# A one-core kernel of a sparse attention layer and a ranked non-local layer: GpSimd takes some relus, scaled sums and squares, mask products follow the relus, ranking tiles become fixed pieces, and the planner's preferences are set anew

## The chip, the cores and the metric

One core of a Trainium2 chip runs the whole program. The metric is the device time in microseconds (us) of one execution. TensorE is called PE here, VectorE DVE, ScalarE ACT, GpSimd POOL and SyncE SP, as in the profile. All data are float32 except some masks and throw-away outputs.

## What is computed

The input x is 2 images of 256 channels and 64x64 = 4096 pixels. Layer 0: a 3x3 convolution to 64 channels, a batch norm and a PReLU give e; the similarity of all pixels, e^T e, is put through a sparsemax along each row (subtract a threshold tau, relu), and x times that matrix is added to x. Layer 1: every pixel gets a vector g of 128 channels and two numbers a and b; y at pixel n is the sum over m of relu(a_n + b_m) g_m / 4096; y is projected back to 256 channels, scaled by a batch norm, and added to the input of the layer.

```
y = where(bn(conv(x)) >= 0, ., prelu * .);  e = y.reshape(B, 64, 4096)
p = relu(sim - tau)          # sim = e^T e, tau: sparsemax threshold of the row
x = x @ p + x
f = relu(a[:, None] + b[None, :]);  y = (f / 4096) @ g
out = bn(wz @ y) + x
```

## The kernel before, in words

**Survey, list, rows.** The kernel counts on almost every row of the sparsemax having one non-zero entry, its own pixel. For each image a *survey* (`survey`, L475) forms the similarity in units of 128 rows by 1024 columns: PE multiplies (L472), DVE keeps a running maximum over the columns (`columns`, L499: a copy L501 for the first row tile, a maximum L503 for the others), ACT sums what lies over the row's limit (L507). The limits come from `thresholds` (L419): PE turns e, ACT copies it, DVE squares (L448) and sums it. `listed` (L580) lists the at most 512 rows that need more, fetches them by indirect DMAs of POOL, and a mask marks all other pixels. `rows` (L728) computes the listed rows in 4 tiles k of 128 rows by 4 column pieces q: PE product, ACT copy to z (L745), DVE top 8 (L748). When the four pieces are there, DVE's `threshold` (L750 to L762; L754 in it is a subtraction on 128x8) gives the bias, and a `relu` (L765) of each 128x1024 piece of z runs on ACT (L768) or on DVE (L770). `doubled` (L713) multiplies x by the mask on POOL, 8 pieces of 128x1024 for each image (L720). `attend` (L787) multiplies z by the fetched columns of x on PE (L794), and DVE adds that into x (L801), for which the piece's mask product must be done.

**Layer 1.** `project` and `project_in` give g, a and b (`ga`). Instead of the full sum, keys b are *ranked* (class `Ranked`): for image 0 all 32 tiles of 128 keys, for image 1 the first 16 tiles. The rank of each key in a tile t is counted by `above` against all keys (L992 on ACT with Sign and a running sum, or L997 on DVE), in two instructions, the keys before and behind the tile, and `ties` (L1004, DVE) counts equal keys inside the tile. `place` adds the counts up, `scatter` writes the tile's rows of `ga` to DRAM in the order of the ranks (an indirect DMA of POOL, L1026). `chain` then loads the sorted table, makes prefix sums (L1052, L1059, L1066), stores them, finds for every pixel the place of its a (`segments` L1086/L1087 on DVE, L1095 on PE, `counts`), and fetches one row of the table per pixel (64 indirect DMAs of POOL, L1112). `scaled_sums` (L1125, DVE) combines its halves, PE turns the result (L1132), and `finish` (L900) projects it with PE (L912), adds x on DVE (L916) and sends it out. The last 16 tiles of keys of image 1 go the direct way: ACT makes f = relu(a + b_m) of 128x1024 (`pair_f`, L1397, 64 of them), PE sums f against g (`pair_py`, L1407), ACT scales the result (L1418).

**The order of the work.** Nothing of it is an order by hand. `Plan` (L94) is a list scheduler that runs while the program is built: every `plan.task` has a cost in us on each engine that may take it (P = PE, D = DVE, A = ACT, G = POOL, S = SP), a rank (its preference; the lower goes first), tasks it comes after, and rings of buffers it takes and frees. At each step the engine that can begin first takes the task that would be least late, and of these the one with the lowest rank; a task with two costs goes to whichever engine picks it first. Instructions are issued in that order, and each engine's queue runs in order on the chip. The costs decide nothing but the order.

**Rings and rooms.** PSUM has 3 buffers of 1024 columns (`ring_sim`) and 2 of 512 (`ring_av`). f has 4 buffers in SBUF, which `ring_f` tells the planner of. Large SBUF rooms S0 to S6 are used several times; `kb` and `tab` of image 0 lie where its z was, and `rest` (L1418) where the throw-away output `junk` of ranking 0 was.

Of the kernel before, what the change touches and what calls it, by code (L numbers as in the profile page):

```python
# [19 lines left out]
P = 128  # L20
# [5 lines left out]
CT = 2  # L26
# [164 lines left out]
def sparse_path(ctx: ExitStack, tc, a, out, rows_i):  # L191
# [88 lines left out]

    plan = Plan()
    ring_sim, ring_av, ring_y, ring_b, ring_f = Ring(3), Ring(2), Ring(2), Ring(2), Ring(4)
# [136 lines left out]
    def thresholds(b, e_of, there, rank):  # L419
# [21 lines left out]

        def limits(jp):
            if jp == 0:
                for n in ("d", "thr", "nthr", "lim"):
                    both[n] = small.tile([P, NT], F32, name=f"{n}_{b}", tag=n, bufs=2)
            es = d[jp, "es"]
            sq = work.tile([P, 2, 4, CR], F32, name=f"sq_{b}_{jp}", tag="wb")
            nc.vector.tensor_mul(sq, es, es)  # L448
            c = both["d"][:, ts(jp, 8)]
            nc.vector.tensor_reduce(c, sq, AX.X, ALU.add)  # L450
            thr = both["thr"][:, ts(jp, 8)]
            nc.vector.tensor_scalar(thr, c, 1.0 - SLACK_REL, -1.0 - SLACK, ALU.mult, ALU.add)
            nc.vector.tensor_scalar_mul(both["nthr"][:, ts(jp, 8)], thr, -1.0)
            lim = both["lim"][:, ts(jp, 8)]
            nc.vector.tensor_scalar(lim, c, 1.5 * SLACK_REL, 1.0 + 1.5 * SLACK, ALU.mult, ALU.add)

        limited, saved = [], []
        for jp in range(NCB // 2):
# [3 lines left out]
            u = plan.task({"D": 2.1}, lambda jp=jp: limits(jp), rank, [t], take=hb, free=[hb])  # L462
            limited.append(u)
            saved.append(plan.task({"S": 0.2}, lambda jp=jp: stored(jp), rank, [t, u], lat=2.6, free=[hy]))
# [10 lines left out]
    def survey(b, e_of, both, there, copied, limited, accs, rank, ready):  # L475
# [23 lines left out]
        def columns(i, q, acc):  # L499
            if i == 0:  # L500
# [28 lines left out]
        def one_unit(i, q):  # L529
# [8 lines left out]
            if q == i // 8:  # L538
                rest.append(plan.task({"D": 1.32, "A": 1.3}, lambda e: own_row(e, i, q), r, [t, limited[i // 8]], free=[h]))
                return  # L540
            acc = accs[q % len(accs)]
            before = [first] + (turns.get(q - len(accs), []) if i == 0 else [chain[q]])
            u = plan.task({"D": 1.3}, lambda: columns(i, q, acc), r, [t, *before])
            chain[q] = u
            rest.append(plan.task({"A": 1.3}, lambda: rows_over(i, q), r, [u, limited[i // 8]], free=[h]))
# [32 lines left out]
        return plan.task({"D": 1.5}, listing, rank - 1, rest + limited), lambda: got_s["flag"], pes  # L578

    def listed(b, et, flag_of, saved, flagged, got, rank, free_mask, free_ec):  # L580
# [116 lines left out]
        pl = T({"D": 4.0}, places, rank, [t], free=[h])  # L697
# [30 lines left out]
    def rows(b, e_of, got, ecs, rank, free_z):  # L728
# [36 lines left out]
        def relu(e, k, q):  # L765
# [3 lines left out]
            else:  # L769
                nc.vector.tensor_scalar(z, z, nbs[k], 0.0, ALU.add, ALU.max)  # L770

        done, pes = {}, []
        for k in range(KB):
# [8 lines left out]
            t = plan.task({"D": 2.0}, lambda k=k: threshold(k), rank - 0.2, tops)  # L782
            for q in range(NU):
                done[k, q] = plan.task({"A": 1.16, "D": 0.8}, lambda e, k=k, q=q: relu(e, k, q), rank - 0.1, [t])
# [115 lines left out]
    def finish(b, cols, scaled, engine, rank, after, free):  # L900
# [27 lines left out]
        for ct in range(CT):  # L928
            t = plan.task({"D": 0.68}, lambda ct=ct: last(ct), rank, [ps[ct]], free=[hz] if ct == CT - 1 else [])
            plan.task({"S": 0.05}, lambda ct=ct: out_of(ct), 50, [t])  # L930

    class Ranked:
# [8 lines left out]
        def __init__(self, b, ga, R, at):  # L941
            self.b, self.ga, self.R, self.at = b, ga, R, at
            self.key = None if ga is None else ga[:, 0:R, CI + 1]
            self.lo, self.hi = 0, R
            self.placed = self.found = 0

        def keys(self):
# [16 lines left out]
            self.junk = None  # L964
            self.cnt = small.tile([P, R, 4], F32, name=f"cnt_{b}", tag=f"cnt{b}")
            nc.vector.memset(self.cnt[:, 0, 0:1], 0.0)
            nc.vector.memset(self.cnt[:, :, 2], 0.0)
# [14 lines left out]
        def above(self, t, on_act):  # L982

            if self.junk is None:
                self.junk = self.at("junk", [P, 2, self.R * P], BF16)
            kb, cnt = self.kb, self.cnt
            n = self.R * P
            for d, (c0, c1) in enumerate(((0, t * P), (t * P, n))):
                if c0 == c1:
                    continue  # L990
                if on_act:
                    nc.scalar.activation(  # L992
                        self.junk[:, 0, c0:c1], kb[:, c0:c1], AF.Sign, scale=STEEP,
                        bias=self.bound[:, d, t : t + 1], accum_out=cnt[:, t, d : d + 1],
                    )
                else:
# [3 lines left out]
                    )  # L1000

        def ties(self, t):

            nc.vector.scalar_tensor_tensor(  # L1004
                self.junk[:, 1, ts(t, P)], self.kb[:, ts(t, P)], self.key[:, t : t + 1], low,
                ALU.is_equal, ALU.mult, accum_out=self.cnt[:, t, 3:4],
            )

        def place(self, t0, n, on_act):

            b, R = self.b, self.R
            cnt = self.cnt[:, ds(t0, n)]
            if on_act:

                nc.vector.memset(cnt[:, :, 2], float(R * P))
            rk = small.tile([P, 4], F32, name=f"rk_{b}_{t0}", tag="rk", bufs=2)
            nc.vector.tensor_reduce(rk[:, 0:n], cnt[:, :, 0:3], AX.X, ALU.add)
            nc.vector.scalar_tensor_tensor(
                self.rank[:, ds(t0, n)], rk[:, 0:n], 0.5 if on_act else 1.0, cnt[:, :, 3], ALU.mult, ALU.add
            )  # L1020
# [98 lines left out]
        def taken(self, i, rank, rest=None):  # L1119
# [3 lines left out]
            def scaled_sums(t):  # L1123
                rt = self.r[:, t % TH]
                nc.vector.scalar_tensor_tensor(  # L1125
# [16 lines left out]
            for t in mine:  # L1142
                u = plan.task({"D": 0.3}, lambda t=t: scaled_sums(t), rank, [self.fetched[t]])
                u = plan.task({"P": 0.14}, lambda t=t: turned(t), rank, [u] + ([v] if t % 4 else []), take=None if t % 4 else h)
                v = u
                if t + TH < NT:
                    self.fetch_task(t + TH, rank, [u])
# [3 lines left out]
        def fetch_task(self, t, rank, after):  # L1151
            self.fetched[t] = plan.task({"G": 1.02}, lambda: self.fetch(t), rank, after, lat=4.14)

        def begin(self, rank, after, ranked, chained, then, room):

            self.chained, self.then, self.ranked = chained, then, ranked
            self.parts = {"D": [], "A": []}
            self.places_done, self.aboves, self.over = [], [], plan.gate()
# [4 lines left out]
            n = self.R / NT  # L1163
            for t in range(self.R):
                self.aboves.append(
                    plan.task(
                        {"D": 4.55 * n, "A": 4.15 * n}, lambda e, t=t: self.ranked_by(e, t),
                        lambda e, t=t: ranked + (t if e == "D" else self.R - t) / 100.0, [sp, *room],
                    )
                )  # L1170

        def ranked_by(self, e, _):
            t = self.hi - 1 if e == "A" else self.lo
            self.lo, self.hi = (self.lo, t) if e == "A" else (t + 1, self.hi)
            self.above(t, e == "A")
            me = self.aboves[_]
            tie = plan.task({"D": 0.3}, lambda: self.ties(t), self.ranked - 0.6, [])
            mine = self.parts[e]
            mine.append((t, me, tie))
            for x, m in self.parts.items():  # L1180
                if m and (len(m) == 4 or self.lo == self.hi):
                    t0, k = min(y[0] for y in m), len(m)
                    deps = [y[1] for y in m] + [y[2] for y in m]
                    pl = plan.task({"D": 0.5 if x == "A" else 0.3}, lambda t0=t0, k=k, x=x: self.place(t0, k, x == "A"), self.ranked - 0.7, deps)
                    for i in range(t0, t0 + k):
                        self.places_done.append(plan.task({"G": 1.02}, lambda i=i: self.scatter(i), self.ranked, [pl], lat=2.3))
                    m.clear()
            if self.lo == self.hi:
                self.chain()

        def chain(self):

            R, b, rk, H = self.R, self.b, self.chained, self.R // TH
            plan.let_go(self.over, self.places_done)
# [5 lines left out]
            for i in range(R // 2):  # L1200
                t = plan.task({"D": 0.82}, lambda i=i: self.sums(2 * i, 2 * i + 2), rk + 0.5, [t])
# [637 lines left out]
```

## Time and profile before

| | us |
|---|---|
| median of 3 runs | 735.35 (734.71 to 736.77) |
| the profiled execution | 737.18 |
| its span, first to last instruction | 735.4 |
| busy: PE / DVE / ACT / POOL | 636.2 / 559.1 / 398.2 / 203.5 |
| granted clock of PE, mean | 0.938 |

The profile's page names lines of the kernel (L754 is line 754) and groups of instructions with their mean length. A view of windows cuts the span into stretches with the busy time of each engine; a timeline lists one engine's instructions with start, length, and in brackets the idle time before them and what ended it; a view of waits adds such idle times up. In the span the stages lie about so: conv of image 0 to 60, survey 0 and conv of image 1 to 200, rows 0 to 262, survey 1 with attend 0 in between to 350, rows 1 with the rest of attend 0 to 440, attend 1 and ranking 0 to 520, ranking 0 and 1 with the pairs to 600, chains, fetches and pairs to 690, the last of `finish` to the end.

### The profile page before, as it was taken

What the parts mean: (1) busy time and instruction counts of PE and PEld (TensorE: products, weight loads), DVE (VectorE), ACT (ScalarE), POOL (GpSimd) and SP (SyncE); (2) the same over time, 40 slices, a digit from 0 to 9 for tenths busy, and PEclk for the clock granted to TensorE, in tenths of its full rate; (3) what the DMA queues carried; (4) which work ended last, traced back from release to release, by engine and by line L of the source; (5) the groups of instructions that cost most, each with busy time, mean ns of one, the idle gap of its engine ahead of it and who ended that gap; (6) DMA issues with size and microseconds to landing.
All of it is one profiled execution on the core that took longest, in us unless ns stands there. A gap on an engine that the chain in (4) does not pass through costs nothing.

```text
span 735.4 us, 8191 instructions
## 1 busy us (share of the span) xinstructions
PE 636.2 (87%) x2783; PEld 312.3 (42%) x2783; DVE 559.1 (76%) x1025; ACT 398.2 (54%) x552; POOL 203.5 (28%) x252
## 2 busy tenths in 40 slices
PE   5989979999876979999897959996798998979683
PEld 4656444444322323333544524445443644534341
DVE  6875787677788998786746485999999987772463
ACT  0122647766555877666031352999999865414010
POOL 0006930000048000000083000152445323777240
PEclk9999999999979899999998969998899899979898
DMA  9512010001021000000110002011425345654364
GB/s 353 185 43 59 2 29 15 15 15 30 15 65 29 1 1 1 0 1 0 59 37 0 0 1 115 8 37 37 138 99 136 98 159 201 218 162 107 129 226 152
DMA packets 32984, 54.75 MB, mean 74 GB/s; under 512 B 12850, under 2 KB 19876, under 8 KB 32036
## 3 DMA queue, kind: packets, MB, share of 16 engines
q1 hardware_dynamic: 27252, 40.60, 16.5%
q0 software_dynamic: 5248, 12.94, 6.5%
q10 hardware_dynamic: 432, 0.59, 0.3%
q8 instruction: 24, 0.39, 0.2%
q14 instruction: 28, 0.23, 0.1%
HBM read 31.94 MB, written 20.07 MB: 71 GB/s over the span
## 4 chain that ended last, share of the span: by engine, by line
PE 50%; DVE 23%; ACT 12%; issue 6%; POOL 4%; DMA 4%; DVEq 0%; ACTq 0%; POOLq 0%; SPq 0%
PE sv L472 16%; ACT junk L992 9%; PE av L794 7%; PE cv_in L362 6%; PE cv_out L362 6%; PE py L1407 4%; DVE junk L997 4%; POOL r L1112 4%; DVE mq L748 4%; DVE xbs L503 4%; PE pz L912 3%; PE g L825 2%; DVE z L754 2%; DMA r<-tb,k 2%; DVE z L770 2%
## 5 line engine op out<-in xcount | busy, mean ns | idle before, releaser
L507 ACT ACTIVATE sv<-sv,nthr 128x1024 f32<-128x1024 f32 x134 | 145.9, 1090 | 93.7 <-DVE xbs L503 47.8
L472 PE MATMUL sv<-e 64*128 64x512 f32 x640 | 162.7, 627 | 7.3 <-ACT sv L507 7.3
L794 PE MATMUL av<-z,xbs 128*128 128x512 f32 x256 | 124.2, 627 | 15.5 <-DVE z L770 15.0
L503 DVE TENSOR_TENSOR xbs<-sv,xbs 128x1024 f32<-128x1024 f32 x90 | 110.1, 1224 | 29.6 <-PE sv L472 24.2
L1407 PE MATMUL py<-f,ga 128*128 128x512 f32 x256 | 120.7, 624 | 3.4 <-ACT f L1397 3.4
L992 ACT ACTIVATE junk<-kb,bound 128x640 bf16<-128x640 f32 (+30 forms) x58 | 96.5, 1665 | 8.7 <-DMA kb<-rd_k 8.7
L1397 ACT ACTIVATE f<-ab,ga 128x1024 f32<-128x1024 f32 x64 | 71.3, 1142 | 47.3 <-PE py L1407 47.2
L472 PEld LDWEIGHTS sv<-e 64*128 64x128 f32 x640 | 55.7, 189 | 92.6 <-ACT sv L507 49.9
L1026 POOL DMA_INDIRECT sg<-ga,rank x48 | 49.9, 1041 | 148.3 <-DVE junk L1004 104.0
L794 PEld LDWEIGHTS av<-z,xbs 128*128 128x128 f32 x256 | 47.5, 197 | 82.4 <-issue 55.6
L1112 POOL DMA_INDIRECT r<-tb,k x64 | 61.2, 957 | 59.1 <-PE yr L1132 20.7
L997 DVE TENSOR_SCALAR_CACHE_REDUCE junk<-kb,ga 128x128 bf16<-128x128 f32 (+29 forms) x36 | 76.6, 2162 | 0.2
L666 POOL DMA_INDIRECT eb<-et,idx x8 | 7.9, 983 | 243.8 <-DVE idx L660 129.2
L1407 PEld LDWEIGHTS py<-f,ga 128*128 128x128 f32 x256 | 49.5, 200 | 59.8 <-issue 52.7
L362 PE MATMUL cv_out<-v,wu 128*64 128x256 f32 (+1 forms) x384 | 48.8, 397 | 7.4 <-DVE v L324 7.4
L362 PE MATMUL cv_in<-v,wu 128*64 128x256 f32 (+1 forms) x384 | 49.0, 398 | 4.9 <-DVE col L524 3.9
L1125 DVE SCALAR_TENSOR_TENSOR r<-r,a 128x128 f32<-128x128 f32 x64 | 21.6, 350 | 31.3 <-DMA r<-tb,k 31.0
L801 DVE SCALAR_TENSOR_TENSOR x<-av,b,x 128x512 f32<-128x512 f32 x32 | 23.7, 747 | 27.7 <-PE av L794 26.1
L745 ACT COPY z<-rw 128x1024 f32<-128x1024 f32 x32 | 30.5, 1026 | 26.1 <-PE av L794 17.3
L362 PEld LDWEIGHTS cv_out<-v,wu 128*64 128x64 f32 x384 | 30.4, 142 | 29.0 <-issue 12.5
L912 PE MATMUL pz<-yT,wz_sb 128*128 128x512 f32 x64 | 33.3, 662 | 9.4 <-DVE yT L1139 8.1
L512 DVE MAX8 top<-sv 128x8 f32<-128x1024 f32 x26 | 32.0, 1231 | 12.2 <-PE sv L472 11.8
(202 smaller groups left out, 752.4 us busy)
## 6 DMA issues: line engine op xcount, KB each, us to landing
out<-x SPq DMA_DIRECT2D x32, 256.0 KB, 2.1
tb<-tab SPq DMA_DIRECT2D x3, 2056.0 KB
x<-in_x SPq DMA_DIRECT2D x8, 512.0 KB, 8.7
tab<-sg SPq DMA_DIRECT2D x3, 1040.0 KB, 7.6
x<-in_x SPq DMA_DIRECT2D x4, 544.0 KB
e<-e SPq DMA_DIRECT2D x16, 128.0 KB, 3.2
et<-es SPq DMA_DIRECT2D x16, 128.0 KB, 1.9
mask<-kd SPq DMA_DIRECT2D x2, 1024.0 KB, 4.6
```

Of the source, the lines that this page charges most:

```text
L362: nc.tensor.matmul(d[jp, g][ts(h, CR), n, (r0 - r) * HH : (r1 - r) * HH], lhsT=taps(j, kc, dy), rhs=v[:, kc, r0 + dy - 1 : r1 + dy - 1], s ...
L472: nc.tensor.matmul(ps[:, ts(h, CB)], lhsT=lhs(h), rhs=e[ts(h, CR), q], start=True, stop=True)
L503: nc.vector.tensor_tensor(out=acc, in0=d[i, q], in1=acc, op=ALU.max)
L507: nc.scalar.activation(ps, ps, AF.Relu, bias=both["nthr"][:, i : i + 1], accum_out=got_s["over"][:, i, q : q + 1])
L794: nc.tensor.matmul(pss[j, ct], lhsT=got["xb"][:, k, ts(ct, P)], rhs=got["zs"][k][:, ts(j, CB)], start=(k == 0), stop=(k == KB - 1),)
L912: nc.tensor.matmul(d["z"][:, ct], lhsT=wz_sb[:, ts(ct, P)], rhs=d["y"], start=True, stop=True)
L992: nc.scalar.activation(self.junk[:, 0, c0:c1], kb[:, c0:c1], AF.Sign, scale=STEEP, bias=self.bound[:, d, t : t + 1], accum_out=cnt[:, t, d ...
L997: nc.vector.tensor_scalar(self.junk[:, 1, c0:c1], kb[:, c0:c1], self.key[:, t : t + 1], None, (ALU.is_ge, ALU.is_gt)[d], ALU.add, accum_ou ...
L1026: rows = nc.gpsimd.indirect_dma_start(out=self.sg, out_offset=bass.IndirectOffsetOnAxis(ap=self.rank[:, t : t + 1], axis=0), in_=self.ga[: ...
L1112: nc.gpsimd.indirect_dma_start(out=self.r[:, t % TH], out_offset=None, in_=self.tb, in_offset=bass.IndirectOffsetOnAxis(ap=self.k[:, t : t ...
L1397: nc.scalar.activation(f[0][:, m % 4, :], ab1[0][:, ts(q, UN)], AF.Relu, bias=ga1[0][:, m, CI : CI + 1])
L1407: nc.tensor.matmul(pys[q][:, ts(h, CB)], lhsT=ga1[0][:, m, 0:CI], rhs=f[0][:, m % 4, ts(h, CB)], start=(m == NR), stop=(m == NT - 1),)
```

## The change

- **Squares**: L448 moves from DVE to POOL, as a task of its own between the ACT copy and the limits.
- **First columns**: the copy of the first row tile (L501) may go to ACT.
- **Relus of z** may also go to POOL, at a planner's cost of 1.3 (`GF`).
- **Mask products** come after all 16 relus of the image (`done.values()`), no longer only after the mask.
- **f** of the pairs may go to POOL as well; the ring of f and the strict order of the f tasks are replaced by a dependence on the fourth `pair_py` back.
- **Scaled sums** may go to POOL, as two instructions (a product and an addition).
- **Ranking tiles as fixed pieces**: before, the engine that took a ranking task chose the tile (ACT from the top end down, DVE from the bottom up), and four tiles of the same engine were placed together. Now each task has its tile, goes to ACT or DVE, and tiles 4i to 4i+3 are placed together; ACT's counts get columns of their own (3 and 4), so `place` has two reductions and a memset for each tile that ACT took.
- **Preferences**: twenty ranks are set anew, and some costs in the planner are nearer to lengths (fetch 1.02 to 1.27, scatter 1.02 to 1.28, turns 0.14 to 0.27). A fetch also waits for the counts of its tile.

```diff
+    GF = 1.3
+    DB, CV1, LS, RW0, SV1, RW1, A0, G0, A1, R0, K0, CH0, R1, K1, CH1, P1, P2, SP1, PY, PF = 6.7, 13.3, -11.03, -18.93, -8.67, 0.74, -7.78, -1.83, -12.57, 4.87, 15.62, -10.51, -8.38, -10.32, 14.63, -1.37, -22.58, -8.67, 14.89, -20.4
+    other = {"D": nc.vector, "G": nc.gpsimd}
...
+        def squared(jp):
+            es = d[jp, "es"]
+            d[jp, "sq"] = work.tile([P, 2, 4, CR], F32, name=f"sq_{b}_{jp}", tag="wb")
+            nc.gpsimd.tensor_mul(d[jp, "sq"], es, es)
...
-            u = plan.task({"D": 2.1}, lambda jp=jp: limits(jp), rank, [t], take=hb, free=[hb])
+            v = plan.task({"G": 1.1}, lambda jp=jp: squared(jp), rank, [t], take=hb)
+            u = plan.task({"D": 1.2}, lambda jp=jp: limits(jp), rank, [v], free=[hb])
...
+            if e == "A":
+                nc.scalar.copy(acc, d[i, q])
...
-                nc.vector.tensor_scalar(z, z, nbs[k], 0.0, ALU.add, ALU.max)
+                other[e].tensor_scalar(z, z, nbs[k], 0.0, ALU.add, ALU.max)
...
-                done[k, q] = plan.task({"A": 1.16, "D": 0.8}, lambda e, k=k, q=q: relu(e, k, q), rank - 0.1, [t])
+                done[k, q] = plan.task({"A": 1.16, "D": 0.8, "G": GF}, lambda e, k=k, q=q: relu(e, k, q), rank - 0.1, [t])
...
+        def place(self, t0):
+
+            b = self.b
+            for t in range(t0, t0 + 4):
+                if t in self.on_act:
+                    nc.vector.memset(self.cnt[:, t, 0:1], float(self.R * P // 2))
+            cnt = self.cnt[:, ds(t0, 4)]
+            rk = small.tile([P, 2, 4], F32, name=f"rk_{b}_{t0}", tag="rk", bufs=2)
+            nc.vector.tensor_reduce(rk[:, 0], cnt[:, :, 0:3], AX.X, ALU.add)
+            nc.vector.tensor_reduce(rk[:, 1], cnt[:, :, 3:5], AX.X, ALU.add)
+            nc.vector.scalar_tensor_tensor(self.rank[:, ds(t0, 4)], rk[:, 1], 0.5, rk[:, 0], ALU.mult, ALU.add)
...
+                if e == "G":
+                    nc.gpsimd.tensor_scalar_mul(rt[:, 0:CI], rt[:, 0:CI], self.a[:, 0, t : t + 1])
+                    nc.gpsimd.tensor_add(rt[:, 0:CI], rt[:, 0:CI], rt[:, CI + 1 : CS])
+                    return
...
+                u = plan.task({"D": 0.35, "G": 0.7 * GF}, lambda e, t=t: scaled_sums(e, t), rank, [self.fetched[t]])
...
-                    self.fetch_task(t + TH, rank, [u])
+                    self.fetch_task(t + TH, rank, [u, self.ks[(t + TH) // 8]])
...
+                r = ranked + t / 100.0
+                u = plan.task(
+                    {"D": 0.25 + 0.00107 * n, "A": 0.66 + 0.00083 * n}, lambda e, t=t: self.above(t, e == "A"), r, [sp, *room]
                 )
+                self.ranked.append(u)
+                places += [u, plan.task({"D": 0.36}, lambda t=t: self.ties(t), r + 0.02, [sp, *room])]
+                if t % 4 == 3:
+                    pl = plan.task({"D": 0.6}, lambda t=t: self.place(t - 3), ranked - 0.7, places)
...
-    halves0 = doubled(0, got[0], masked0, raw0, -5)
+    halves0 = doubled(0, got[0], masked0, list(done0.values()), DB)
...
-    projected0 = project(0, ga0_of, last0, -10.5)
+    projected0 = project(0, ga0_of, last0, G0)
...
-    r0.begin(-7.93, [turn0], 7.11, 9.11, {"ab": a_of_0, "rest": None}, rw1)
+    r0.begin(R0, [turn0], K0, CH0, {"ab": a_of_0, "rest": None}, rw1)
...
+        if e == "A":
+            nc.scalar.activation(fm, am, AF.Relu, bias=bm)
+        else:
+            nc.gpsimd.tensor_scalar(fm, am, bm, 0.0, ALU.add, ALU.max)
...
-            t = plan.task({"A": 1.08}, lambda q=q, m=m: pair_f(q, m), -4, [spread1[q], projected[m]] + prev, take=hf)
+            t = plan.task({"A": 1.14, "G": GF}, lambda e, q=q, m=m: pair_f(e, q, m), PF, [spread1[q], projected[m]] + prev[-4:-3])
...
-        -9, [projected[NR - 1]], 10.13, 6.74,
+        R1, [projected[NR - 1]], K1, CH1,
```

The old and new ranks that the prediction speaks of: project 0 -10.5 to -1.83; the pieces of ranking 0 7.11 to 15.62 and of ranking 1 10.13 to -10.32; chain 0 9.11 to -10.51 and chain 1 6.74 to 14.63; f -4 to -20.4; the projection of image 1 1 and -6.53 to -1.37 and -22.58.

## The prediction

> **What bounds the kernel now.** I read the page first, then the windows (busy time by stage), then PE's waits and the timelines around the longest of them.
>
> ```profile
> span 735.4 us, 8191 instructions
> PE 636.2 (87%) x2783; PEld 312.3 (42%) x2783; DVE 559.1 (76%) x1025; ACT 398.2 (54%) x552; POOL 203.5 (28%) x252
> ```
>
> The change takes nothing from PE. So the span can only fall by what PE idles, 735.4 - 636.2 = 99.2 us, and by the slow spells that follow idling. The windows (stretch, length, busy us of PE, PEld, DVE, ACT, POOL, granted clock, DMA) say where the idling is:
>
> ```profile
> 200.00:265.00 65.00, 51.27 (x200) 18.58 (x196) 59.46 (x96) 40.50 (x57) 24.67 (x16) 0.87 0.10 27
> 350.00:440.00 90.00, 74.27 (x296) 38.26 (x295) 57.71 (x105) 26.77 (x32) 24.73 (x18) 0.90 0.07 20
> 440.00:520.00 80.00, 67.59 (x230) 36.74 (x229) 69.39 (x146) 65.56 (x70) 21.27 (x41) 0.93 0.14 50
> 520.00:600.00 80.00, 75.56 (x231) 39.51 (x231) 75.49 (x177) 72.70 (x93) 32.95 (x55) 0.93 0.39 113
> 600.00:690.00 90.00, 77.08 (x235) 38.18 (x233) 57.89 (x120) 33.91 (x31) 53.70 (x56) 0.92 0.55 173
> 690.00:736.00 46.00, 29.15 (x90) 14.26 (x90) 24.02 (x42) 3.37 (x6) 7.55 (x8) 0.87 0.54 185
> ```
>
> PE idles 13.7, 15.7, 12.4, 4.4, 12.9 and 16.9 us here, and some 24 us before 200 and in survey 1. From 520 to 600 DVE (75.5 of 80) and ACT (72.7) are full at once, and POOL has 47 us free. PE's waits name the longest single causes:
>
> ```profile
> PE av L794 <- DVE z L770: 15.0, 4, 5.4
> PE pt_a L876 <- DVE cnt L1015: 7.2, 1, 7.2
> ```
>
> The 15.0 us begin in `threshold`, where DVE's timeline and POOL's belong together:
>
> ```profile
> 230.41 6.95 DVE L754 TENSOR_SCALAR z<-m 128x8 f32<-128x8 f32 x1
> ...
> 245.19 0.23 DVE L754 TENSOR_SCALAR z<-m 128x8 f32<-128x8 f32 x1
> ```
>
> ```profile
> 224.79 12.54 POOL L720 TENSOR_TENSOR x<-x,mask 128x1024 f32<-128x1024 f32 x6
> ```
>
> ```profile
> 239.15 3.78 PE L794 MATMUL av<-z,xbs 128*128 128x512 f32 x4 [5.43 <-DVE z L770]
> ...
> 250.80 1.98 PE L794 MATMUL av<-z,xbs 128*128 128x512 f32 x4
> ```
>
> A subtraction on 8 columns takes 0.23 us, and 6.95 when POOL is in its run of mask products; it ends at 237.36, as that run does at 237.33. Image 1 repeats it (6.70 at 386.33, POOL's run ending at 393.00). So some DVE instructions cannot run beside POOL's arithmetic, and they wait for a whole run of it, not for one instruction. L383, an addition of two SBUF tiles, shows the same: 4.10 us, against 0.41 for its neighbour L384. Maxima over PSUM (L503) and MAX8 (L748) ran beside POOL unharmed.
>
> **The change, part by part**, against this execution's span of 735.4.
>
> *Mask products behind the relus.* L754 no longer meets them: 6.95 + 6.70 - 2 x 0.23 = 13.2 us off the chain. PE sees 5.43 us of waiting before 239.15 and 4.34 before 396.06, and after the first the same four matmuls take 3.78 us instead of 1.98, so 5.43 + 1.8 + 4.34 + 1.5 = 13.1, the same sum. Given back: the products (8 x 2.13 = 17.0 us an image) now begin after the last relu, and the first `into` waits for the first, about 2.3 us; an image's two first blocks of `attend` (3.4 us each) fill PSUM's two buffers and cover part of it; later products (2.13 each, one per two blocks) stay ahead. I take 1.5 an image. Late next is DVE's own MAX8, 4.60 us a tile. Term: -13 + 3 = **-10** (bounds -13 and 0).
>
> *Relus on POOL.* A tile's turn on DVE is 7.3 to 8.1 us (L754 at 245.19, 252.60, 260.66): 4.60 of MAX8, 1.4 of threshold, 1.4 to 2.1 of relus (0.75 each; ACT 1.16). The trace shows no such relu on POOL. From below, MEMSET 1x257 takes 0.32 and 1x1 0.09, so 0.9 ns a column, 1.0 us for 1024; from above the two-input product takes 2.13. A relu reads one tile: I take 1.3, nearer the lower row. One DVE relu fewer a tile is 0.67 x 8 = 5.4; but the relus left on DVE may be of the kind that waits for POOL, up to 1.3 each. **-4** (-12 to +10).
>
> The Trainium skill's page "GPSIMD Engine Reference", section "Engine selection", calls one-input work on GpSimd roughly line-rate; at its 1.2 GHz that is an estimate of 0.85 us plus dispatch for 1024 columns, within my bounds.
>
> *f on POOL.* ACT makes 36 of the 64 f before 592, 1.07 us apart, while it and DVE share the ranking. If POOL takes 15 of them, 16 us of ACT come free, and as a ranking piece goes to either engine the stage shortens by half, **-8** (-20 if POOL takes all that its 47 free us hold, 36 x 1.07 / 2; 0 if PE's sums, 1.72 us an f, are late anyway: between 600 and 621 ACT waits for PE before every f).
>
> *Squares, first columns.* Eight squares of 0.77 leave DVE, where it is busy 73 of 100 us, with about 1.1 us of POOL (L329: 1.02 for 128x512) in the chain to the limits, which ACT's sums need only later; six copies of 1.22 may go to ACT. PE idles 5.4 us in 100 to 200: **0** (-3 to +3).
>
> *Fixed pieces.* Twelve `place` instead of 14, each with one more reduction (0.16) and about one more memset (0.06): 12 x 0.61 - 14 x 0.39 = 1.9 us of DVE, shared with ACT: **+1** (0 to +2).
>
> *Scaled sums on POOL.* DVE's 0.35 each are not late (it is busy 58 of 90 us). On POOL two passes over 128 columns cost 0.5 to 0.8 (0.28 for L324's 16 columns, 2.1 ns a column for two inputs). The fetches go out there without a gap from 615.87 to 686.33, 56 x 1.258 us, so each sum taken in that run delays the rest: **+2** (-2 to +10).
>
> *Preferences.* (a) 500 to 520: PE waits 7.2 + 1.3 + 3.2 = 11.7 us, mostly for L862, which stands behind a 4.7 us ranking piece that cannot be broken off. The projection of image 1 goes further ahead, the piece stays as long: -4. (b) The tail: fetches begin at 615.87 and last 70 us, so 13 blocks of `finish` are left after 690, each 1.8 us of PE with waits between. Ranking 1 is now ahead: 16 pieces of 2.4 us on two engines with 16 ties are some 25 us after its keys (516.5), to 542; its chain takes 34 us (last scatter 595, first raise ended 630), so its 32 fetches could start near 576 instead of after image 0's, and POOL's stream would end some 20 us earlier. Then PE is late next, with the 12.9 + 16.9 - 10 (the last write and drain, from 725.5) = 19.8 us that it idles after 600. I take about half, -11. Together **-15** (-35 if the tail's idling goes and f start earlier; +20 if ranking 0, put last with its 85 us of two engines, delays its chain by as much as ranking 1 gains, less 5).
>
> *Contention.* DVE's instructions on two SBUF tiles or short `tensor_scalar`s are 48 ties, 32 of L1086/L1087, 48 of L1052/L1059 and 64 scaled sums, about 190. With POOL's f at 15 x 1.3 = 20 us of the 80, a quarter of them meets one and waits half of 1.3: 190 x 0.25 x 0.65 = 31, of which a third falls while DVE is late: **+10** (0, to +45 if POOL takes 36 f and DVE stands still through all 36 x 1.3 of them). POOL's scatter also stretches beside DVE: 2.86 us instead of 0.96 at 563.02, while L1052 ran.
>
> The Trainium skill's page "SBUF — State Buffer", section "Who interferes with whom", states an exclusive lock between GpSimd and such VectorE instructions, held for one instruction. The 6.95 us above are more than one product's 2.13, so the trace is harsher. By the rule a DVE instruction loses one f at most, so the 15 f could cost 15 x 1.3 = 20 us and the sum would end at -14 or better; by the trace one wait may last a whole run, which leaves the wider bound.
>
> Sum: -10 - 4 - 8 + 0 + 1 + 2 - 15 + 10 = -24, so a span of **711.4**. The median of the runs shown (735.35) equals the span of the profiled execution (735.4), whose own time was 737.18; I forecast 711 for the median.
>
> **Rivals.** *The order gains more* (18%): the tail's idling goes and contention stays near 3: -24 - 12 - 7, some 692. For it: PE's 29.8 idle us after 600 and POOL's free time; against: PE must still be 636 busy, and 24 us of idling lie where nothing changes. *Gain and contention cancel* (14%): -10 from the masks stays, the rest gives 5 and contention 3: 733; also if POOL takes next to none of the work. *POOL holds DVE up* (16%), slower: the place is the ranking stage, DVE's ties, sums and segments behind runs of f and relus; a run of four holds DVE 5.2 us as L754 was held, and 16 such runs are 83 us at worst. It decides from 34 us of contention (24 + 10), about 0.2 us for each of the 190; at 55 us the span is 735 - 34 + 55 = 756, at half that excess about 746, which I take. For it: 6.95 and 4.10 us above. Against: f is paced by PE at 1.72 us, so runs on POOL are short, and L997, the bulk of DVE there, ran untouched beside POOL's scatters.
>
> **Numbers.** Forecast (700 to 726) 52%, more gain 18%, cancelled 14%, slower 16%. The measurement can tell 0.3%, 733.1 to 737.6. Faster: 52 + 18 + 8 of the cancelled = 78%; same 6%; slower 16%. For 8 in 10 the range leaves out the lower half of the second case and the upper part of the last: 690 to 744. It takes in each unknown alone at its bound (contention at +45 gives 746, order at -35 gives 691).
>
> **What would show it.** L754 at 0.23 eight times, and PE not waiting 5.4 us for L770; POOL's 128x1024 relus near 1.3; in ranking, ACT with fewer f; DVE rows with maxima several times their median (ties, L1087, L1059) if contention is large; the first fetch of an image before 600; PE idling near 75 in all. Wrong if POOL's relu costs 2 us or more, if L754's kin are held elsewhere, or if PE idles more before 440, where conv 1 and project 0 now come last.

## The result, and the profile after

The changed kernel takes **756.45 us** (756.09 to 757.83) against 735.03 (734.29 to 736.77) for the kernel before: a ratio of **1.029 [1.027, 1.031]**. The forecast was 711 us, and its range ended at 744. The profiled execution took 757.83 us, with a span of 756.1.

The kernels ran on several chips. In the runs of this result and in set B below the kernel before takes about 735, in the other sets more. There its single runs spread from 743 to 761, and the ratios below leave out those over 1.5% above its fastest; the medians of the rest are 752.2, 736.2, 747.1, 747.7 and 747.3 us in sets A to E. Up to the first fetch the traces of one kernel agree within some 3 us (the changed kernel's first fetch starts at 625.1 and 627.8 us where it takes 757, at 628.4 where it takes 783). Behind it the slower chips stand still at times on waits that the trace can put down to nothing ("remote", "issue"). So times are compared inside one set of runs only, and across sets one thing: **how much PE has worked in the first 600 us**, which is 530.0 and 529.6 us in two executions of the kernel before. Two executions of one kernel can be further apart: "all relus back" has 529.0 and 525.1 below, with 2476 and 2479 matmuls. So differences of up to 4 us by this measure say nothing.

The head of the page after, and its three groups of relus on GpSimd and of f on ACT (busy us, mean ns of one, then idle time before them):

```profile
span 756.1 us, 8251 instructions
PE 640.9 (85%) x2783; PEld 308.8 (41%) x2783; DVE 542.0 (72%) x1035; ACT 393.4 (52%) x536; POOL 310.3 (41%) x292
L1399 ACT ACTIVATE f<-ab,ga 128x1024 f32<-128x1024 f32 x49 | 56.1, 1148 | 101.5 <-PE py L1409 93.4
L1401 POOL TENSOR_SCALAR f<-ab,ga 128x1024 f32<-128x1024 f32 x15 | 55.8, 3726 | 30.0 <-ACT f L1399 28.8
L781 POOL TENSOR_SCALAR z<-z,nb 128x1024 f32<-128x1024 f32 x9 | 37.1, 4126 | 66.4 <-ACT z L756 34.3
```

A relu of 128x1024 takes POOL 3.73 us in f and 4.13 in z. The prediction took 1.3 and bounded it at 2.13; the plan was made with 1.3 too. DVE is busy 17 us less than before, ACT 5 less, POOL 107 more.

The windows after (the last is 67 us long, where the one of before was 46):

```profile
200.00:265.00 65.00, 53.29 (x198) 19.64 (x200) 58.48 (x83) 48.81 (x72) 36.24 (x18) 0.89 0.05 10
350.00:440.00 90.00, 72.10 (x308) 37.74 (x307) 60.70 (x105) 43.87 (x48) 38.03 (x19) 0.87 0.12 38
440.00:520.00 80.00, 64.31 (x223) 35.27 (x222) 75.00 (x172) 64.44 (x67) 41.91 (x66) 0.89 0.10 31
520.00:600.00 80.00, 59.88 (x170) 28.74 (x168) 52.09 (x135) 42.75 (x59) 67.37 (x49) 0.85 0.38 109
600.00:690.00 90.00, 76.08 (x240) 39.19 (x240) 63.75 (x122) 31.88 (x32) 53.22 (x48) 0.92 0.51 170
690.00:757.00 67.00, 48.55 (x126) 21.71 (x126) 22.46 (x45) 14.80 (x13) 21.35 (x27) 0.88 0.38 120
```

From 520 to 600 the roles are exchanged: DVE and ACT, full before, are busy 52 and 43 of 80 us, POOL is at 67, and PE has lost 15.7 us (75.56 to 59.88). The loss of 20.7 us of span adds up from three parts: by 600 PE has done 516.2 us of work instead of 530.0 (13.7), its whole work is 4.7 us longer (matmuls behind a wait run slower: four of L1409 take 3.60 after a wait of 3.95, otherwise 1.98), and it idles 31.5 us after 600 instead of 29.2 (2.3).

POOL's timeline of that stage and one row of PE's show how (start, length, operation, idle time before):

```profile
544.06 0.97 POOL L1039 DMA_INDIRECT sg<-ga,rank  x1 [0.23 <-issue]
545.07 14.91 POOL L1401 TENSOR_SCALAR f<-ab,ga 128x1024 f32<-128x1024 f32 x4
559.92 0.09 POOL L1038 MEMSET gap<- 1x1 f32 x1
560.17 1.08 POOL L1039 DMA_INDIRECT sg<-ga,rank  x1 [0.16 <-issue]
```

```profile
548.83 3.60 PE L1409 MATMUL py<-f,ga 128*128 128x512 f32 x4 [3.95 <-POOL f L1401]
```

Four f in a row keep PE waiting for L1401, and a scatter, whose ranks are ready at 543.2, stands 15 us behind them. That scatter belongs to ranking 1. The chain of image 0, which goes first, is late in two ways. PE's matmuls for its segments (L1108) stand in PE's queue behind `py`, so DVE waits 5.7 and 6.1 us for them, with the prefix sums behind it in its own queue. And a load that image 0's segments need goes out at 594.6, right behind that of ranking 1's table in SyncE's queue (592.4), which needs the last scatter (590.1); DVE waits another 5.3 us for it. The matmul that closes image 0's prefix sums (`po`) shows it, before and after:

```profile
597.62 0.67 PE L1063 MATMUL po<-tab,tri 128*128 128x257 f32 x2 [0.63 <-PE pk L1095]
```

```profile
607.05 0.60 PE L1076 MATMUL po<-tab,tri 128*128 128x257 f32 x2
```

So the fetches start at 625.1 instead of 615.9. PE's waits over the whole span:

```profile
PE av L805 <- DVE x L812: 13.2, 6, 6.3
PE av L805 <- DVE z L781: 11.3, 3, 6.2
PE py L1409 <- POOL f L1401: 9.3, 5, 4.0
PE pt_a L887 <- DVE ga L873: 8.8, 1, 8.8
```

The wait of 15.0 for z is down to 11.3 only, that of 7.2 at `pt_a` is now 8.8, and 13.2 for `into` (L812) and 9.3 for POOL's f are new. In the rows stage the threshold itself (L754 before, L765 now) is free, as predicted. DVE's and POOL's timelines together:

```profile
223.30 0.23 DVE L765 TENSOR_SCALAR z<-m 128x8 f32<-128x8 f32 x1
...
224.44 2.28 DVE L781 TENSOR_SCALAR z<-z,nb 128x1024 f32<-128x1024 f32 x2
...
231.50 0.23 DVE L765 TENSOR_SCALAR z<-m 128x8 f32<-128x8 f32 x1
```

```profile
224.58 4.20 POOL L781 TENSOR_SCALAR z<-z,nb 128x1024 f32<-128x1024 f32 x1 [12.01 <-DVE nb L773]
...
249.15 4.19 POOL L781 TENSOR_SCALAR z<-z,nb 128x1024 f32<-128x1024 f32 x1 [4.01 <-DVE nb L773]
253.31 16.75 POOL L731 TENSOR_TENSOR x<-x,mask 128x1024 f32<-128x1024 f32 x8
```

L765 is at 0.23 all eight times. But two DVE relus beside POOL's one take 2.28 instead of 1.42, and a tile's turn is 8.20 us (223.30 to 231.50) where it was 7.41 to 8.06. In image 1 the last tile has two relus on POOL (7.84 us from 422.48), and the mask products wait behind them until 430.30; PE's longest wait for `into`, 6.3 us before 433.25, is for the first of these products.

### The profile page after: what moved, and what is told of

It reads as the page before. It is cut to its first block, busy times and chain, and to the rows that moved or that the text cites. A ratio compares the mean times of both kernels' runs of the same rounds, so it can differ in the third digit from the quotient of the medians.

```text
span 756.1 us, 8251 instructions
## 1 busy us (share of the span) xinstructions
PE 640.9 (85%) x2783; PEld 308.8 (41%) x2783; DVE 542.0 (72%) x1035; ACT 393.4 (52%) x536; POOL 310.3 (41%) x292
## 4 chain that ended last, share of the span: by engine, by line
PE 53%; DVE 24%; POOL 12%; issue 5%; DMA 4%; ACT 1%; SPq 0%; DVEq 0%; POOLq 0%; ACTq 0%
PE sv L478 17%; PE av L805 10%; PE py L1409 7%; PE cv_in L365 6%; POOL f L1401 6%; PE cv_out L365 6%; DVE mq L759 4%; DVE junk L1004 4%; POOL r L1125 3%; DVE xbs L511 3%; DMA r<-tb,k 3%; DVE z L781 2%; PE g L836 2%; PE pz L923 2%; POOL sg L1039 2%
## 5 line engine op out<-in xcount | busy, mean ns | idle before, releaser
L515 ACT ACTIVATE sv<-sv,nthr 128x1024 f32<-128x1024 f32 x130 | 141.5, 1089 | 73.2 <-DVE xbs L511 40.9
L805 PE MATMUL av<-z,xbs 128*128 128x512 f32 x256 | 130.6, 653 | 29.2 <-DVE x L812 13.2
L1409 PE MATMUL py<-f,ga 128*128 128x512 f32 x256 | 130.2, 657 | 13.2 <-POOL f L1401 9.3
L999 ACT ACTIVATE junk<-kb,bound 128x1152 bf16<-128x1152 f32 (+30 forms) x62 | 108.2, 1746 | 7.5 <-DMA kb<-rd_k 6.6
L1399 ACT ACTIVATE f<-ab,ga 128x1024 f32<-128x1024 f32 x49 | 56.1, 1148 | 101.5 <-PE py L1409 93.4
L1409 PEld LDWEIGHTS py<-f,ga 128*128 128x128 f32 x256 | 51.4, 211 | 72.3 <-issue 52.9
L1401 POOL TENSOR_SCALAR f<-ab,ga 128x1024 f32<-128x1024 f32 x15 | 55.8, 3726 | 30.0 <-ACT f L1399 28.8
L1004 DVE TENSOR_SCALAR_CACHE_REDUCE junk<-kb,ga 128x256 bf16<-128x256 f32 (+22 forms) x32 | 63.1, 2010 | 5.2 <-DMA kb<-rd_k 4.7
L781 POOL TENSOR_SCALAR z<-z,nb 128x1024 f32<-128x1024 f32 x9 | 37.1, 4126 | 66.4 <-ACT z L756 34.3
L448 POOL TENSOR_TENSOR sq<-es 128x512 f32<-128x512 f32 x8 | 8.9, 1114 | 132.8 <-ACT es L439 132.8
L520 DVE MAX8 top<-sv 128x8 f32<-128x1024 f32 x30 | 37.0, 1233 | 22.2 <-PE sv L478 22.2
```

Of the source, the lines that this page charges most:

```text
L515: nc.scalar.activation(ps, ps, AF.Relu, bias=both["nthr"][:, i : i + 1], accum_out=got_s["over"][:, i, q : q + 1])
L805: nc.tensor.matmul(pss[j, ct], lhsT=got["xb"][:, k, ts(ct, P)], rhs=got["zs"][k][:, ts(j, CB)], start=(k == 0), stop=(k == KB - 1),)
L999: nc.scalar.activation(self.junk[:, 0, c0:c1], kb[:, c0:c1], AF.Sign, scale=STEEP, bias=self.bound[:, d, t : t + 1], accum_out=cnt[:, t, 3 ...
L1004: nc.vector.tensor_scalar(self.junk[:, 1, c0:c1], kb[:, c0:c1], self.key[:, t : t + 1], None, (ALU.is_ge, ALU.is_gt)[d], ALU.add, accum_ou ...
L1399: nc.scalar.activation(fm, am, AF.Relu, bias=bm)
L1401: nc.gpsimd.tensor_scalar(fm, am, bm, 0.0, ALU.add, ALU.max)
```

## The experiments

Theories at the outset: the *price* of GpSimd's relu carries the loss; the *order* (the new preferences) is bad by itself; *contention* of DVE with POOL. The table has every run but that of the single forms, and the short ones leave work out; "by 600" is PE's busy time before 600 us.

| set | run | time, us | ratio to before | by 600 |
|---|---|---|---|---|
| A | short relus | 752.8 | 1.002 [0.999, 1.005] | 529.5 |
| A | f on ACT | 760.0 | 1.011 [1.004, 1.018] | 524.0 |
| A | all relus back | 754.9 | 1.003 [1.000, 1.006] | 529.0 |
| B | before, again | 735.8 | 1.001 [0.999, 1.003] | 529.6 |
| B | after, again | 757.9 | 1.030 [1.026, 1.034] | 516.1 |
| B | masks moved in the plan | 735.4 | 0.999 [0.997, 1.001] | 533.1 |
| B | true price | 730.7 | 0.992 [0.989, 0.995] | 533.4 |
| C | short relus | 751.0 | 1.004 [1.000, 1.008] | 531.8 |
| C | all relus back | 755.8 | 1.010 [1.004, 1.017] | 525.1 |
| C | masks held, both images | 755.8 | 1.013 [1.005, 1.020] | 528.6 |
| C | price 99 | 876.7 | 1.172 [1.165, 1.179] | 455.5 |
| D | after | 783.4 | 1.044 [1.026, 1.062] | 513.9 |
| D | short relus | 750.9 | 1.004 [0.999, 1.008] | 531.8 |
| D | f short only | 759.5 | 1.013 [0.997, 1.030] | 522.8 |
| D | masks held, image 0 | 741.6 | 0.989 [0.972, 1.006] | 538.0 |
| E | true price | 761.6 | 1.015 [1.009, 1.022] | 533.1 |
| E | true price, z off POOL, masks held | 753.4 | 1.008 [1.003, 1.012] | 533.2 |

### The disputed cost by itself

```
g.tensor_scalar(o1, a1, ptr, 0.0, ALU.add, ALU.max)      # L68; then one form after another
```

> The layers are left out: four of each GpSimd form on 128x1024 float32, one after the other, then relus and products of GpSimd beside DVE. If the length comes from the two operations in one instruction: addition alone and maximum alone at half of 3.7. If it comes from the scalar that is read from SBUF: immediate forms near 1.0, pointer forms near 3.7. If any tensor_scalar is slow on GpSimd: all of them near 3.7, the two-input addition at 2.1 and the copy near 1. Beside DVE: the relu 4.1 and DVE's relu 1.5 to 2.3 instead of 0.75 if they share; if the lock is held over a run, one DVE instruction of 10 to 20 us.

POOL's timeline, four of each form. In order: relu with the column from SBUF (L68), addition alone (L70), maximum alone (L71), relu with immediates (L72), copy (L74), two inputs (L75), addition of a broadcast column as second input (L76), and the relu on 128, 320 and 512 columns:

```profile
5.97 15.08 POOL L68 TENSOR_SCALAR o<-s,ptr 128x1024 f32<-128x1024 f32 x4 [5.53 <-DMA s<-in_x]
...
36.31 11.66 POOL L70 TENSOR_SCALAR o<-s,ptr 128x1024 f32<-128x1024 f32 x4
48.05 11.31 POOL L71 TENSOR_SCALAR o<-s 128x1024 f32<-128x1024 f32 x4
59.45 14.76 POOL L72 TENSOR_SCALAR o<-s 128x1024 f32<-128x1024 f32 x4
...
86.03 4.34 POOL L74 COPY o<-s 128x1024 f32<-128x1024 f32 x4
90.45 9.58 POOL L75 TENSOR_TENSOR o<-s,s 128x1024 f32<-128x1024 f32 x4
100.12 7.80 POOL L76 TENSOR_TENSOR o<-s,ptr 128x1024 f32<-128x1024 f32 x4
...
112.05 3.14 POOL L78 TENSOR_SCALAR o<-s,ptr 128x128 f32<-128x128 f32 x4
115.28 5.69 POOL L79 TENSOR_SCALAR o<-s,ptr 128x320 f32<-128x320 f32 x4
121.07 8.25 POOL L80 TENSOR_SCALAR o<-s,ptr 128x512 f32<-128x512 f32 x4
```

The relu takes 3.70 us, with immediates 3.63, one operation alone 2.76 to 2.84, a copy 1.04. So every `tensor_scalar` that was tried is slow on POOL: one operation costs 1.7 to 1.8 us more than a copy, the second 0.9 more; where its scalar comes from hardly matters. Length: 3.33 ns a column ((1.99 - 0.72) / 384). A sum of *two* tiles (2.34) is cheaper than a sum of *one* tile and a scalar (2.84). The Trainium skill ("GPSIMD Engine Reference", section "Engine selection") calls one-input work roughly line-rate: the copy's 1.04 us fits that, the relu's 3.70 does not.

### Price against order

Short relus: the order of the changed kernel, POOL's relus cut, and one memset on DVE (2.4 us) that gives the columns of f left out a value.

```diff
+                z = z[:, 0:320] if e == "G" else z
...
+            nc.vector.memset(f[0][:, :, 320:UN], 0.0)
...
-            nc.gpsimd.tensor_scalar(fm, am, bm, 0.0, ALU.add, ALU.max)
+            nc.gpsimd.tensor_scalar(fm[:, 0:320], am[:, 0:320], bm, 0.0, ALU.add, ALU.max)
```

> The order of every queue is that of the changed kernel; only the 24 relus that GpSimd takes (9 of z, 15 of f) cover the first 320 of their 1024 columns, so that one should take about 1.2 to 1.4 us, the price the plan was made with, instead of 3.7. The other 704 columns are left out (z keeps its raw values there, f keeps old ones), so the output is not the reference's. Price theory: 24 x 2.4 = 58 us of GpSimd go, PE's idle time falls from 115 to 75 to 95 us, and the time falls to 712 to 736. Order theory (the new preferences are bad by themselves): PE still waits as long, 748 to 756. Contention theory (DVE is held up by GpSimd as such): in between, 738 to 748, with DVE's ties still several times their length.

> The changed kernel's order with short relus on GpSimd (320 of 1024 columns; the rest is left out) once more, since the chip of the first run took 752 us for the kernel before and had stalls of 10 to 16 us in which several engines stood still at once. Price theory: where the kernel before takes 735, this takes 718 to 736, PE's idle time 80 to 97 us, and the 20 us that PE idles in 520 to 600 fall to 8 or less. Order theory: 748 to 756.

Set A left the question open, since its chip took 752 us for the kernel before; so both kernels were run again (set B), and the changed kernel beside the short relus (set D).

> The kernel before, unchanged, beside the others of this call: its profile on this chip is wanted, as the chip of the first runs took 752 us for it where the earlier one took 735. If the chip is slower in one thing (transfers, say), the trace shows those instructions longer and the others the same; the kernel against itself must give a ratio of 1.00.

> The changed kernel, unchanged, on the chip of these runs. If the loss is the same everywhere, 1.03 of the kernel before beside it; if the chip that made the kernel before slower leaves this one as it was, 1.00 to 1.01. The runs with short relus (750.7) and with all relus back (755.0) are to be held against this span, not against 756.1 of the other chip.

> The changed kernel unchanged, beside the run with short relus. Price theory: 15 to 25 us above it. Order theory: within 4 us of it. Against the kernel before: 1.03 where that takes 735; where that takes 750, about 1.02 to 1.03 as well if the slow chip stretches all alike.

> The same order with all 24 GpSimd relus cut to 320 columns (the rest left out). Price theory: 15 to 25 us below the changed kernel beside it, 72 of 80 us of PE in 520 to 600 instead of 60, ratio to the kernel before 0.995 to 1.005. Order theory: within 4 us of the changed kernel.

In set D the same order takes 783.4 us with full relus and 750.9 with short ones: **32.5 us** (27 to 36 by the extremes of both), more than was expected for the price. By 600 it is 17.9 us of PE's work (513.9 against 531.8); the rest lies behind the first fetch, where this chip stalls, and short relus were not run on a chip where the whole loss is 21 to 22 us. The times of 712 to 736 that the price theory expected in sets A and C were not reached (752.8 and 751.0), nor was PE's idle time of at most 97 us (111 to 114 in the three runs): both had been worked out from the chip that takes 735. The window 520 to 600 of the short relus in set D, where the changed kernel beside it has 59.95 for PE:

```profile
520.00:600.00 80.00, 73.14 (x239) 37.98 (x238) 72.23 (x173) 50.59 (x66) 38.86 (x46) 0.96 0.47 143
```

The price theory stands, and the order theory falls as the cause of the loss: short relus (1.49 us an f, 1.80 a z, still above 1.3) are level with the kernel before in A, C and D. On these chips, then, the order also *gains* nothing, where the prediction gave everything but contention -34. Short relus shorten DVE's waits for POOL too, so this pair alone does not part price from contention. PE's waits speak for the price: they name POOL's own f, and DVE is busy for only 52 of 80 us in that stage. With z left raw the values of x, and so the rows that are scattered and fetched, differ as well; the next run leaves x as it is.

Which relus? f alone cut:

> Only the 15 f are cut to 320 columns (the rest left out); the 9 relus of z keep 1024. If f carries the loss, since the scatters of both rankings stand behind it in GpSimd's queue: within 5 us of the run with all short. If the relus of z carry it (each tile turn 8.2 us instead of 7.6, the last tile with two of them, the mask products behind): within 6 us of the changed kernel.

759.5: 23.9 us below the changed kernel, 8.6 above all short. **f carries about three quarters of the time** in this set. By 600 it is half, 8.9 of 17.9 us (522.8). The last scatter shows the part of POOL's queue: it starts at 590.1 in the changed kernel, at 573.4 with f short and at 563.0 with all short. Moved instead of cut, at the same places of the order (`e = "A"` at the head of `pair_f`; and for all relus back also `e = "D" if e == "G" else e` in `relu`):

> The plan is that of the changed kernel, but the 15 f that went to GpSimd are issued on ACT at the same places of the order. ACT gets 15 x 1.15 = 17 us more in a stage where it is busy 43 of 80 us. If f in GpSimd's queue is the main loss (it holds the scatters of both rankings): PE's idle time in 520 to 600 falls from 20 to some 5 us and the end comes earlier by as much, 730 to 742. If the z relus carry more of it: 745 to 752. If the preferences do: 752 to 760, with the waits moved to ACT.

> The plan of the changed kernel again, with its 15 f issued on ACT and its 9 z relus on DVE; nothing of 1024 columns but the mask products is left on GpSimd. Price theory: within 1% of the run with short relus, 715 to 738, that is about before or better. Order theory: 748 to 756, as the preferences stay. The part that the z relus carry is this run less the one with only f moved: 3 to 10 us by the waits of attend on z (11.3 us) and the mask products behind them (13.2 us).

> The changed kernel's order with its 15 f issued on ACT and its 9 z relus on DVE, once more. Price theory: 722 to 740. As nothing of GpSimd stands ahead of the mask products any more, they run before the relus in spite of the plan (5.71 us of one threshold in the first run), so 3 to 8 us more than with short relus. Order theory: 748 to 756.

In set A, f on ACT leaves 7.2 us more than short relus, and z back on DVE takes 5.1 of that away, so z's part is 5.1 us there, where it was 8.6 in set D. "All relus back" is 2.1 us (A, within the spread of both) and 4.9 us (C) behind "short relus": its mask products run ahead of the relus again (a threshold of 5.71 us in set A, 6.14 in set C), as expected.

### The true price told to the planner

```diff
-    GF = 1.3
+    GF = 3.75
```

> The changed kernel with the planner told 3.75 us for a relu on GpSimd instead of 1.3 (0.91 for a scaled sum as before), the preferences as they are; the planner is free to leave relus to ACT and DVE. Price theory: most relus go back and PE idles 80 to 95 us, so 0.97 to 0.985 of the changed kernel. Order theory: within 0.5% of the run with all relus back, which is the changed kernel less some 5 us at most.

> The changed kernel with the planner told 3.75 us for a relu on GpSimd, once more, as it is the best so far (0.9922 of the kernel before where that takes 736). Expected again 0.985 to 0.996 of the kernel before beside it.

> The changed kernel planned with a price of 99 us for a relu on GpSimd, so that none goes there (scaled sums at 0.91 as before), the new preferences kept. With the true price the time was 730.7. If GpSimd's relus help at their true price: 733 to 742 here. If they cost more than they bring: 722 to 729. If the masks, which then run free, give back the threshold's stretch, some 5 us are of that.

Told the true length, the planner still gives POOL 8 relus of z and 11 f, but puts other work around them: 730.7 us, 0.964 of the changed kernel beside it and 0.8% better than the kernel before on that chip. The expectation that most relus go back was wrong: a task goes to the engine that can *begin* first, and the price only says until when that engine is taken. That is also why 99 us kept 2 z and 3 f on POOL and, as the list then held POOL for taken 99 us after each, planned the rest around a fiction: PE waits 73.3 us for `into` at one place. That run tells nothing of the preferences. In set E the true price is 1.015 of the kernel before, although PE has done 533.1 us by 600 as on the fast chip (533.4). So this version is not faster on every chip; its last fetch starts at 728.6 us there and at 706.9 on the fast chip, and why is open.

### Where the mask products' gain went

In the plan alone (`halves0` after `rows`, with `list(done0.values())`, both images), on the kernel before:

> The kernel before with one part of the change: the mask products come after all relus of their image, ranks and everything else as they were. The term of the prediction: -10 us (bounds -13 and 0), so 0.982 to 1.000 of before, most likely 0.986. Rival: the masks then stand between the last relu and the first into, and the waits come back there, ratio 0.998 to 1.01.

0.999 [0.997, 1.001], and the first threshold is as long as ever:

```profile
231.80 7.51 DVE L754 TENSOR_SCALAR z<-m 128x8 f32<-128x8 f32 x1
```

```profile
222.57 16.71 POOL L720 TENSOR_TENSOR x<-x,mask 128x1024 f32<-128x1024 f32 x8
```

"After" in the plan is only a place in the list. The products read nothing of the relus, so POOL, with nothing ahead of them in its queue, runs them as before. In the changed kernel it was POOL's own relus, standing ahead of them, that held them. A real dependence:

```diff
+        def held():
+            last = small.tile([P, KB], F32, name=f"last_{b}", tag="last", bufs=2)
+            zv = got["zs"][KB - 1].rearrange("p (q n) -> p q n", q=NU)
+            nc.gpsimd.tensor_copy(last, zv[:, :, UN - 1])
...
+        t = plan.task({"G": 0.2}, held, rank, [masked, *raw])
```

The products then come after `t`.

> The kernel before with mask products that really wait: GpSimd first copies the last column of the four relu pieces of the image's last tile (128x4), which it can't do before they are done. In the run with the masks moved in the plan alone GpSimd ran them as early as before, 7.51 us of a threshold included, since they read nothing of the relus. If the prediction's term is right: threshold at 0.23 eight times and 722 to 732 (ratio 0.982 to 0.995). If the waits come back at the first additions into x: 733 to 740.

> The kernel before with the mask products of image 0 alone held behind its relus; image 1 as before. The prediction's term says half of 13 less 1.5, that is -5 us; if nothing behind gives it back, 0.989 to 0.996 of the kernel before. If the gain only moves a later wait: 0.998 to 1.003.

Held in both images, the thresholds take 0.23, and the last tile of image 1 comes at 425.99 on PE instead of 437.41 (the kernel before in set B): 11.4 us won. Then DVE's keys of ranking 0 meet the products, and PE waits for the keys:

```profile
433.88 2.20 DVE L957 TENSOR_TENSOR keys<-ga 128x32 f32<-128x32 f32 x1
436.11 8.49 DVE L958 TENSOR_SCALAR keys<-keys 128x32 f32<-128x32 f32 x1
```

```profile
436.22 8.34 POOL L720 TENSOR_TENSOR x<-x,mask 128x1024 f32<-128x1024 f32 x4
```

```profile
445.61 0.37 PE L882 MATMUL pt_k<-ident,ga 128*32 128x128 f32 x1 [11.31 <-DVE ga L964]
```

L882 starts at 445.61 where the same step (L876) started at 444.96 before: all of it given back. Held in image 0 alone, the same step starts at 435.36, and PE has done 538.0 us by 600, 8 more than before. The time is 741.6 us (739.3 to 742.4) against 744.0 to 754.2, but the kernel before spreads so widely there that the interval takes in 1. So the wait that the prediction named can be won in image 0, by PE's work before 600; in time it is not shown, and held in both images it is lost again.

> True price for f, no relu of z on GpSimd at all, and the mask products held by a copy of four columns of the last tile's relus, so that thresholds still take 0.23 us. If GpSimd's relus of z only lengthened the tiles' turns (8.2 us against 7.4 with DVE and ACT alone): 4 to 8 us less than the run with the true price. If they took load off DVE and ACT that is missed: 3 us or more above it. If the new order of tasks spoils the end of the span, as lists of this kind may do on any edit, the windows after 520 show it and the stage 200 to 265 is compared alone.

8.1 us below the true price beside it, where 4 to 8 were expected; but the rows stage (53.46 us of PE from 200 to 265 against 53.32) and the sum by 600 are level, so the difference arose behind 600 and the reason given for it is not shown.

## Why the prediction was wrong, point by point

- **The step that failed first: relus on POOL.** "From above the two-input product takes 2.13. A relu reads one tile: I take 1.3." The length was bounded by rows of *other* operations, on the belief that fewer inputs cost less. It is 3.70 alone, 3.73 and 4.13 in the kernel, outside the bounds: 15 x 2.43 + 9 x 2.83 = 62 us of POOL that neither the plan nor the sum knew. The term of -4 (at worst +10) for the relus of z became a loss, 8.6 us for their length by the run with f short (set D), 5.1 against DVE by the runs of set A. The prediction named its own sign of this, "Wrong if POOL's relu costs 2 us or more". Of `tensor_scalar` on POOL the trace of before has only L324, 16 columns wide, and the prediction used that row for the scaled sums alone.
- **f on POOL, -8**: the same length in the same sum, a loss of about 24 us in set D (8.9 of it by 600), as scatters and PE's `py` stand behind f. Even at a fair price the -8 could not be had: the window of before shows PE idle for 4.4 us from 520 to 600. A term may not exceed what PE idles where it is claimed.
- **Masks, -10**: the threshold at 0.23 is right, the sum wrong. Tile turns of 8.2, the products behind POOL's relus (6.3 us of the 13.2 for `into`) and ties that meet them (L1018 up to 2.21 us where its median is 0.35) took it back. The prediction also took "after" for a wait.
- **Preferences, -15**: part (a) moved, 8.8 instead of 7.2 us at `pt_a`. Part (b): the first fetch does come earlier when the price is right (598 to 602 with short relus or the true price, 615.9 before), but image 0 goes first, not image 1; and on the fast chips PE idles 31.5 us after 600 in the changed kernel and 29.6 at the true price, against 29.2 before. An earlier start did not shorten the tail. With the plan made at 1.3 the last 48 matmuls of `py` come behind the last fetch (717.4 to 738.2 in the changed kernel, 711.8 to 732.6 with short relus in set D); at the true price they do not, but the last fetch still starts only at 706.9, against 715.2 before.
- **Contention, +10**: too large by its own count. It took 31 us of waiting for DVE and a third of that for the span; the four kinds it counts became 11 us longer (ties 4.4, segments 3.7, prefix sums and scaled sums 1.5 each). The relus of z left on DVE lost another 6.9 (1.18 us instead of 0.75 each). What of this reached the span was not measured.
- **Squares, pieces, scaled sums**: none was run alone. PE idles 7.0 us from 100 to 200 where it was 5.4, and POOL took 4 scaled sums at 1.02 us or a little more each, where the prediction had 0.5 to 0.8.
- **The rival "POOL holds DVE up"** named 756 us at its far end. That the number fits is chance, for the mechanism was another: DVE was less busy, and PE waited for POOL's own results.

So -24 fell to about nothing without the price (short relus are level with before on the slower chips), and the price made the rest.

## What to carry to other kernels

Before work moves to another engine, measure that very instruction there: rows of other operations, even costlier-looking ones, are no bound. Cap each gain by what the bounding engine idles in that window, and ask what stands behind the moved work in its new engine's queue, since a long instruction delays the short ones that others wait for. An order in a plan holds nothing back on the chip unless a queue or a dependence does, and a wait removed may return at the next instruction that meets the same engine.

## What the runs showed that was not expected

POOL's `tensor_scalar` is slower than its `tensor_tensor` at the same width (3.70 and 2.84 against 2.34 alone in the forms run). And how long DVE stands behind POOL varies. In the forms run, 1024-column DVE relus beside POOL's two-input sums take turns with them (median 2.71 us, POOL's 2.67), which is what the Trainium skill ("SBUF — State Buffer", section "Who interferes with whom") says of a lock held for one instruction. Beside POOL's relu the same DVE relus hardly wait: their median stays at 0.75 us (1.48 at most), and POOL's take up to 4.68 instead of 3.70. In the run with masks held L957 waited for one product (2.20 us), but L958 right behind it for four (8.49), and in the kernel before L754 for a whole run. What decides between one and a run was not found; nor what the slower chips wait for behind the first fetch.
